# Attention and a quantized network on one core: the scores run one unit further ahead, six product pairs of the network's first group move between attention's last products, and the start and the end are joined differently

## The chip, the core and the metric

The kernel runs on one core of a Trainium2 chip. The core has four engines that compute, each with its own queue of instructions: TensorE (PE; "PEld" is its loading of the stationary operand), VectorE (DVE), ScalarE (ACT) and GpSimd (POOL). SyncE (SP) issues all DMA transfers of this kernel, in one queue. The metric is the time of one execution on the device in microseconds (us); lower is better.

## The reference

Sixteen sequences of 256 tokens with 256 values each go through one attention layer and one network layer, both with the norm before and after and with the input added:

```python
x = x + layernorm(attn(layernorm(x), W_Q, W_K, W_V, W_O, b_Q, b_K, b_V, b_O))
x = x + layernorm(ffn(layernorm(x), gate, up, down))
```

`attn` has 16 heads of 128, a causal mask and a softmax. `ffn` unpacks 4-bit codes with one scale for 32 values into the weights of gate, up (2048 x 256) and down (256 x 2048), and computes `(gelu(x @ gate.T) * (x @ up.T)) @ down.T`. Everything is float32.

## The kernel before

**Precision.** TensorE takes most operands as pairs: a high part (fp32r) and the low rest. A product of two such pairs is three matmuls (high x high, high x low, low x high), which `mm3` (line 353) issues. Six matmuls of 512 columns are the common piece of work ("a product" below).

**Order.** `run` (line 95) issues every instruction behind all issued before it, so each engine's queue has the order of the program, and all instructions have line 99 in the profile; they are told apart by their tiles. `dma` (line 86) does the same for SP, with line 91. Small jobs (norms, unpacking of weights) are generators in lanes; at places called `slot` (line 133) one step of the first lane whose step is for the wanted engine is put into the program. `finish`, `await_` and the loops in `product` (line 762) and `f_get` (line 666) force steps when the data is needed.

**Attention.** Tokens are handled in 8 blocks of 512 (two sequences). For each block, its 16 heads are 16 units: 128 units in all, two to a pair. The main loop (line 952) runs `i` from -4. In iteration i it issues, in this order: scores of unit i+3 (`st_s`, tiles sc, pr), queries and keys of unit i+4 (`st_qk`, two products, tiles pk, pq), the 32x32 turn of the probabilities of i+3 (`st_t`, tr), half of the output product of the pair before (`st_o`, po, tile wo), the weighted values of unit i (`st_z`, pz, zh, zl), the split of the probabilities of i+1 (`st_p`, ph, pl), values (`st_v`, pv), and on SP the load of the turned probabilities of i+2 (`st_b`, hop to pt) and the four stores of those of i+3 (`st_w`, tr to hop). Then come weights: in odd iterations wk and wq of pair p+4, in even ones wo of pair p and half of wv of p+4 (line 990). Blocks after the first take their weights, already split, from a copy in HBM that `w_keep` wrote. A block's normed, turned and split tokens are the tile xT (`ln1`, line 231; `first_tokens`, line 245, for the first block).

**Weights of the network.** From pair 7 of the first block on, `f_make` (line 598) unpacks one of 24 pieces at a time in the lane `idle`, on VectorE (codes, sg, t, v), and `f_scale` scales and splits it on GpSimd and ScalarE. `f_load` (line 590) loads the packed codes (tile ld).

**Network.** Blocks are taken two at a time and the products of gate and up are done by a scheme with seven products in place of eight. `x_ops` (line 684) makes seven combinations of the tokens; class `Two` (line 754) has the seven products m1 to m7, each for gate ("g") and up ("u") with three matmuls (tiles pa, pd, pf, pe). Products of one name are a "pair" below. Their sums, GELU and splits wait in the list `pending` and are issued one or two at a time by `part` (line 830); `quarter` (line 841) issues those that a down product needs. There are 32 groups (4 pairs of blocks, 8 groups of 256 hidden values each). The loop at line 1008 issues the products of group k and between them the four down products (`st_d`, line 850) of group k-1, which add up in four banks of PSUM. In attention's last three iterations m1, m2 and m6 of group 0 are issued after the iteration's other work (line 997).

**End.** After the last group each of the last two blocks is copied from PSUM whole, turned on TensorE, normed, added to the input and stored (`end_now`, line 897).

## Time and profile before

| what | value |
| --- | --- |
| time, median of 3 runs | 1543.86 us (1541.33 to 1545.67) |
| profiled execution, its own time | 1548.52 us |
| its span, first to last instruction | 1546.7 us |
| instructions | 25648 |
| busy: PE / PEld / DVE / ACT / POOL | 1510.8 / 1281.4 / 1178.4 / 1033.0 / 810.1 us |
| mean granted TensorE clock | 0.991 |
| moved by DMA | 407.55 MB, mean 263 GB/s |
| first product of attention (pk) | 10.87 us |
| attention's last output product | ends near 1045 us |
| last apply of the norm on DVE | 1541.67 us |

The page of the profile gives the busy time of each engine and, in 40 slices, its share. The view of waits names for each engine and tile what ended its idle time. The timeline lists instructions with start, duration, engine, line, operation, tiles (written <- read) and, in brackets, idle time of the engine before it and what ended it. The table of stretches gives for a stretch of time the busy time of each engine with its count of instructions, then the granted clock of TensorE (1.00 is full speed), the share of time in which the 16 DMA engines moved data, and GB/s.

### The profile page before, as it was taken

The numbers are of one execution on the slowest core, as the hardware profiler recorded it, in microseconds if no ns is written. First come the engines' busy times: TensorE is split into PE (matmuls) and PEld (weight loads), VectorE is DVE, ScalarE is ACT, GpSimd is POOL, SyncE is SP. The second block draws the span as 40 slices with busy tenths as digits, with TensorE's granted clock in tenths as the row PEclk, the third lists the DMA queues.
The fourth block names the chain that finished last, engine by engine and source line by source line (L and its number), as shares of the span: only waits on it lengthen the run. The fifth ranks groups of instructions, "written<-read, shape, count | busy, mean of one in ns | idle before, by whom it ended". The sixth has DMA issues, their size and how long they took to land.

```text
span 1546.7 us, 25648 instructions
## 1 busy us (share of the span) xinstructions
PE 1510.8 (98%) x7792; PEld 1281.4 (83%) x7792; DVE 1178.4 (76%) x2944; ACT 1033.0 (67%) x2600; POOL 810.1 (52%) x1017
## 2 busy tenths in 40 slices
PE   8999999999999999999999999989999999999996
PEld 7888888888888888888888888877788878878884
DVE  6875878788788788878777777847777777787765
ACT  6876667767767676676675777656666665665663
POOL 3754669568667767766866866861420330240100
PEclk9999999999999999999999999989999999999999
DMA  8998899989899999899899889975547456655551
GB/s 276 335 310 257 249 303 302 313 293 300 280 293 317 291 310 296 267 326 309 266 315 294 287 281 322 324 238 204 216 179 275 185 220 212 236 192 214 218 195 42
DMA packets 200411, 407.55 MB, mean 263 GB/s; under 512 B 21457, under 2 KB 128465, under 8 KB 189521
## 3 DMA queue, kind: packets, MB, share of 16 engines
q1 hardware_dynamic: 200272, 405.91, 78.6%
q8 instruction: 62, 1.02, 0.3%
q14 instruction: 77, 0.62, 0.1%
HBM read 294.15 MB, written 111.67 MB: 262 GB/s over the span
## 4 chain that ended last, share of the span: by engine, by line
PE 80%; DMA 6%; DVE 5%; ACT 4%; SPq 2%; issue 1%; POOL 0%; DVEq 0%; POOLq 0%; ACTq 0%
PE pd L99 11%; PE po L99 10%; PE pk L99 10%; PE pv L99 10%; PE pq L99 9%; PE pz L99 9%; PE sc L99 8%; PE pa L99 7%; PE pf L99 5%; DVE sum L99 3%; DMA wo<-wo 2%; PE pe L99 2%; SPq L91 2%; ACT inter L99 1%; DMA hop<-tr 1%
## 5 line engine op out<-in xcount | busy, mean ns | idle before, releaser
L99 POOL TENSOR_SCALAR pr<-pr,rc 128x128 f32<-128x128 f32 (+1 forms) x512 | 251.7, 508 | 80.8 <-DVE rc L99 80.8
L99 POOL TENSOR_TENSOR pl<-pt,ph 128x512 fp32r<-128x512 f32 x128 | 165.3, 1291 | 218.3 <-ACT ph L99 211.8
L99 ACT ACTIVATE pr<-sc,mn 128x128 f32<-128x128 f32 (+1 forms) x512 | 208.9, 421 | 83.1 <-DVE mn L99 81.7
L99 DVE CUSTOM_DVE_ANT_0 sc<-sc,mask 128x128 f32<-128x128 f32 (+1 forms) x512 | 180.7, 373 | 63.5 <-PE sc L99 54.7
L99 PE MATMUL pv<-wv,xT 128*128 128x512 f32 x768 | 208.9, 407 | 0.0
L99 PE MATMUL pd<-inter,wd 128*128 128x512 f32 x768 | 199.5, 393 | 5.2 <-ACT inter L99 4.0
L99 PE MATMUL pk<-xT,wk 128*128 128x512 f32 x768 | 201.5, 398 | 1.6 <-ACT wv L99 1.4
L99 PE MATMUL pq<-xT,wq 128*128 128x512 f32 x768 | 196.4, 391 | 0.0
L99 ACT ACTIVATE zh<-pz,bqk 128x512 fp32r<-128x512 f32 x128 | 88.5, 692 | 160.6 <-PE pz L99 160.6
L99 POOL TENSOR_TENSOR rs<-rs,mhalf 128x4 f32<-128x4 f32 (+1 forms) x33 | 35.1, 1065 | 288.5 <-DVE rs L99 287.2
L99 PEld LDWEIGHTS pd<-inter,wd 128*128 128x128 f32 x768 | 142.3, 188 | 42.5 <-DVE inter L99 7.0
L99 PEld LDWEIGHTS pq<-xT,wq 128*128 128x128 f32 x768 | 144.5, 188 | 32.9
L99 PE MATMUL po<-zh,wo 128*128 128x512 f32 x512 | 160.3, 394 | 8.4 <-DMA wo<-wo 8.4
L99 PEld LDWEIGHTS pk<-xT,wk 128*128 128x128 f32 x768 | 136.5, 190 | 25.5 <-ACT xT L99 1.6
L99 PEld LDWEIGHTS pv<-wv,xT 128*128 128x128 f32 x768 | 135.0, 189 | 23.6
L99 DVE SCALAR_TENSOR_TENSOR zl<-pz,bqk,zh 128x512 fp32r<-128x512 f32 x128 | 95.2, 744 | 76.9 <-ACT zh L99 76.7
L99 ACT COPY part<-pa 128x512 f32<-128x512 f32 x192 | 111.9, 586 | 62.4 <-PE pa L99 59.8
L99 ACT CAST inter<-sum 128x512 fp32r<-128x512 f32 x128 | 80.1, 626 | 101.1 <-DVE sum L99 100.9
L99 DVE TENSOR_TENSOR inter<-sum,inter 128x512 fp32r<-128x512 f32 x128 | 92.1, 720 | 58.9 <-ACT inter L99 56.0
L99 DVE STREAM_TRANSPOSE tr<-pr 128x768 f32<-128x768 f32 x128 | 123.3, 963 | 1.1
L99 PEld LDWEIGHTS po<-zh,wo 128*128 128x128 f32 x512 | 96.1, 189 | 31.1 <-DMA wo<-wo 11.5
L99 DVE SCALAR_TENSOR_TENSOR kl<-pk,bqk,kh 128x512 fp32r<-128x512 f32 x128 | 96.0, 750 | 30.3 <-ACT kr L99 27.1
(139 smaller groups left out, 3792.6 us busy)
## 6 DMA issues: line engine op xcount, KB each, us to landing
hop<-tr SPq DMA_DIRECT2D x512, 96.0 KB
pt<-hop SPq DMA_DIRECT2D x128, 384.0 KB
wk<-wk SPq DMA_DIRECT2D x64, 512.0 KB
wq<-wq SPq DMA_DIRECT2D x64, 512.0 KB
wo<-wo SPq DMA_DIRECT2D x64, 512.0 KB
wu<-fu SPq DMA_DIRECT2D x32, 1024.0 KB
wg<-fg SPq DMA_DIRECT2D x32, 1024.0 KB
wv<-wv SPq DMA_DIRECT2D x56, 512.0 KB
```

The lines of the kernel that those rows point to most:

```text
L91: queue[0] = nc.sync.dma_start(dst, src).ins
L99: ins = op(dst, *args, **kw)
```

## The change

1. *Start.* `first_tokens`: all four norms on VectorE, ahead of the split of wk; the split of wq after the turned tokens. 30 warming transposes in place of 24, and 3 and 6 more behind the turns. The low part of the first wv is made on VectorE. In pk and pq the two matmuls with low tokens come last.
2. *Lead.* The loop starts at i = -5; scores, turn and stores are of unit i+4, queries and keys of i+5, the load of the probabilities of i+3, into three buffers of pt instead of two. wk and wq are loaded in even iterations (the same lead over their use), wo of pair p+1 and wv of p+5 in odd ones.
3. *Unpacking.* The first packed codes are loaded one pair (two iterations) earlier. `code` has three buffers instead of four, and v is not begun before the piece before it has been scaled.
4. *Hand-over.* In attention's last six iterations m1, m2, m6, m5, m7, m3 of group 0 stand in front of the output products and the weighted values; group 0 puts some of its intermediate copies into the buffers of pr and tr.
5. *End.* m4 of the last group goes ahead of two down products of the group before. The last group's four down products go by half blocks of 256 tokens (`st_last`), each copied, turned, normed, added and stored while the next is multiplied; all pending operations are issued first. The last half block is stored in two parts.

The core of the diff:

```diff
 # first_tokens
-        w_split(0, "k")
         xn = wide("xn")
-        nb = ln_shift(*stats[1], 2)
-        for t in range(2):
-            mv, rs = stats[0]
+        for t in range(4):
+            mv, rs = stats[t // 2]
             run(nc.vector.tensor_scalar, ...)
-        for t in range(2):
-            ln_apply_act(xn[:, 2 + t, :], xs[1][:, t, :], nb, stats[1][1], t)
-        w_split(0, "q")
+        w_split(0, "k")
...
+            keep_warm(3 + 3 * hf)
             run(nc.scalar.copy, hi, tp)
             run(nc.vector.tensor_tensor, lo, tp, f(hi), ALU.subtract)
+        w_split(0, "q")
 # mm3, with lows_last=True in st_qk
+        if lows_last:
+            todo = [todo[m] for m in (0, 1, 3, 4, 2, 5)]
 # st_b
-        pt = work.tile([P, 4, 6, 32], F32, tag="pt", name="pt")
+        pt = work.tile([P, 4, 6, 32], F32, tag="pt", name="pt", bufs=3)
 # f_make, f_scale
+        while unscaled:
+            step(made)
+        v = small_tile(BF16, "v")
...
+        unscaled.append((g, n))
...
             run(nc.gpsimd.tensor_tensor, full, v, scb, ALU.mult)
+            unscaled.remove((g, n))
 # the main loop
-    for i in range(-4, N + 2):
+    for i in range(-5, N + 2):
...
-            if b == 0 and g == 7:
+            if b == 0 and g == 6:
                 pieces = [(fg, n) for fg in range(NG) for n in "gud"]
                 f_load(*pieces[0])
+            if b == 0 and g == 7:
                 for m, piece in enumerate(pieces):
...
-            st_s(i + 3)
+            st_s(i + 4)
-            st_qk(i + 4)
+            st_qk(i + 5)
-            st_t(i + 3)
+            st_t(i + 4)
+        if i == N:
+            X[0].pop("last")()
+        if i >= N - 4:
+            part(0, ("m1", "m2", "m6", "m5", "m7", "m3")[i - (N - 4)])
...
-            st_b(i + 2)
+            st_b(i + 3)
-            st_w(i + 3)
+            st_w(i + 4)
         if odd:
+            weights((p + 1, "o"), (p + 5, "v"))
+        else:
             weights((p + 4, "k"), (p + 4, "q"))
-        else:
-            weights((p, "o"), (p + 4, "v"))
...
-        if i >= N - 3:
-            for name in (("m1",), ("m2",), ("m6",), (), ())[i - (N - 3)]:
-                part(0, name)
 # the loop over groups (m5, m7, m3 of group 0 left out here too)
+        if k == NGRP - 1:
+            parts(k, "m4")
         st_d(k - 1, 0, 0)
...
-        parts(k, "m4")
+        if k < NGRP - 1:
+            parts(k, "m4")
         st_d(k - 1, 0, 1)
...
     finish(urgent)
+    finish(behind)
+    st_last()
```

The new end, in its own words: `st_last` issues what is pending, then for n = 0 to 5

```python
            if n < count:
                multiply(n, 0)
            if 0 <= n - 1 < count:
                turn_and_measure(n - 1)
            if n < count:
                multiply(n, 1)
            if n >= 2:
                apply(n - 2)
```

with n counting the half blocks (1,0), (1,1), (0,0), (0,1). `multiply` adds six matmuls of 256 columns to the bank and copies the half to SBUF on ScalarE; `turn_and_measure` does four transposes and the statistics; `apply` is one operation on VectorE and one on ScalarE for each 128 tokens, and the store.

More of the change, by code (lines that the diff above doesn't have):

```diff
@@ L251, in first_tokens @@
             stats.append((yield from ln_stats([xs[hf][:, t, :] for t in range(2)])))
-        w_split(0, "k")
         xn = wide("xn")
-        nb = ln_shift(*stats[1], 2)
-        for t in range(2):
-            mv, rs = stats[0]
+        for t in range(4):
+            mv, rs = stats[t // 2]
             run(
                 nc.vector.tensor_scalar,
-                xn[:, t, :], xs[0][:, t, :], mv[:, t, 0:1], rs[:, t : t + 1], ALU.subtract, ALU.mult,
-            )
-        for t in range(2):
-            ln_apply_act(xn[:, 2 + t, :], xs[1][:, t, :], nb, stats[1][1], t)
-        w_split(0, "q")
+                xn[:, t, :], xs[t // 2][:, t % 2, :], mv[:, t % 2, 0:1], rs[:, t % 2 : t % 2 + 1],
+                ALU.subtract, ALU.mult,
+            )
+        w_split(0, "k")
         xt = XT[1, 0] = work.tile([P, 2, 2, TB], F32R, tag="xT", name="xT", bufs=4)
@@ L312, in w_split @@
         run(nc.scalar.activation, wv_[:, 0], raw, AF.Copy, scale=c)
-        if n in "vo":
+        if n in "vo" and (p, n) != (0, "v"):
             run(nc.gpsimd.tensor_tensor, wv_[:, 1], raw, f(wv_[:, 0]), ALU.subtract)
@@ L351, with mm3 @@
     STATIONARY_LAST = ((0, 0), (0, 1), (1, 0))
-    def mm3(o, terms, passes=STATIONARY_LAST, start=True, stop=True, shared=False):
+    def mm3(o, terms, passes=STATIONARY_LAST, start=True, stop=True, shared=False, lows_last=False):
         todo = [(lhs(a), rhs(c)) for lhs, rhs in terms for a, c in passes]
+        if lows_last:
+            todo = [todo[m] for m in (0, 1, 3, 4, 2, 5)]
         for i, (lhs, rhs) in enumerate(todo):
@@ L378, in st_qk @@
         pk = ps.tile([P, TB], F32, tag="pk", name="pk")
-        mm3(pk, [(lambda a, kt=kt: wk_[:, a, kt, cols], lambda c, kt=kt: xt[:, c, kt, :]) for kt in range(2)], MOVING_LAST)
+        mm3(pk, [(lambda a, kt=kt: wk_[:, a, kt, cols], lambda c, kt=kt: xt[:, c, kt, :]) for kt in range(2)], MOVING_LAST, lows_last=True)
         kh = work.tile([P, TB], F32R, tag="kh", name="kh")
@@ L389, in st_qk @@
         pq = ps.tile([P, TB], F32, tag="pq", name="pq")
-        mm3(pq, [(lambda a, kt=kt: wq_[:, a, kt, cols], lambda c, kt=kt: xt[:, c, kt, :]) for kt in range(2)], MOVING_LAST)
+        mm3(pq, [(lambda a, kt=kt: wq_[:, a, kt, cols], lambda c, kt=kt: xt[:, c, kt, :]) for kt in range(2)], MOVING_LAST, lows_last=True)
         qh = work.tile([P, 2, P], F32R, tag="qh", name="qh")
@@ L588 @@
     LD = {}
+    unscaled = []
     def f_load(g, n):
@@ L603, in small_tile @@
         def small_tile(dtype, name):
-            return work.tile([P, 2, 256], dtype, tag="code", name=name, bufs=4)
+            return work.tile([P, 2, 256], dtype, tag="code", name=name, bufs=3)
         c = work.tile([P, 2, 256], I32, tag="raw", name="codes", bufs=6)
-        sg, t, v = small_tile(BF16, "sg"), small_tile(BF16, "t"), small_tile(BF16, "v")
+        sg, t = small_tile(BF16, "sg"), small_tile(BF16, "t")
         run(nc.vector.tensor_scalar, c[:, 0, :], pk, 15, None, ALU.bitwise_and)
@@ L638, in f_scale @@
             run(nc.gpsimd.tensor_tensor, full[:, 0:4].rearrange("p (k c) n -> p k (c n)", k=2), v, scb, ALU.mult)
+            unscaled.remove((g, n))
             w = f_tile("u")
@@ L770, in copy @@
         def copy(self, bank, tag, bufs=2):
-            t = sb_tile(tag, "part", bufs)
+            if self.k == 0 and tag in ("zh", "zl"):
+                t = work.tile([P, 3, D], F32, tag="pr" if tag == "zh" else "tr", name="part").rearrange("p a b -> p (a b)")
+                t = t[:, 0:TB]
+            else:
+                t = sb_tile(tag, "part", bufs)
             run(nc.scalar.copy, t, bank)
@@ L868, in st_d @@
         if g == NG - 1:
-            if sb < NSB - 1:
-                if dh == 0:
-                    ACC[b] = back_tile()
-                back(ACC[b], dh, po)
-                if dh == 1:
-                    add((urgent, behind)[bb], end(b, ACC.pop(b)), N_)
-            else:
-                if dh == 0:
-                    ACC[b] = wide("oT").rearrange("p a b -> p (a b)").rearrange("p (h n) -> p h n", h=2)
-                run(nc.scalar.copy, ACC[b][:, dh], po)
-                if dh == 1:
-                    add(urgent, end_now(b, ACC.pop(b), tags), V_)
+            if dh == 0:
+                ACC[b] = back_tile()
+            back(ACC[b], dh, po)
+            if dh == 1:
+                add((urgent, behind)[bb], end(b, ACC.pop(b)), N_)
     def end(b, tr):
@@ L895, in end, with st_last, multiply, turn_and_measure @@
             dma(half(out, b, hf), X1[b][hf])
-    def end_now(b, oT, tags):
-        yield V_
-        tp = []
-        for hf in range(2):
-            tp.append(ps.tile([P, 2, D], F32, tag=tags[hf], name="tpo"))
+    def st_last():
+        k = NGRP - 1
+        while pending:
+            run(*pending.popleft())
+        w = FW[k, "d"]
+        halves = [(bb, hf) for bb in (1, 0) for hf in range(2)]
+        oTs, os, stats = {}, {}, {}
+        def multiply(n, dh):
+            bb, hf = halves[n]
+            tok = slice(hf * S, (hf + 1) * S)
+            cols = slice(dh * P, (dh + 1) * P)
+            i = [quarter(k, c, bb) for c in range(2)]
+            po = ACC[2 * NSB - 2 + bb, dh][:, tok]
+            mm3(
+                po, [(lambda a, c=c: w[:, a, c, cols], lambda s, c=c: i[c][:, s, tok]) for c in range(2)], MOVING_LAST,
+                start=False, shared=True,
+            )
+            if dh == 0:
+                oTs[n] = wide("oT").rearrange("p a b -> p (a b)")[:, 0 : 2 * S].rearrange("p (h n) -> p h n", h=2)
+            run(nc.scalar.copy, oTs[n][:, dh], po)
+        def turn_and_measure(n):
+            tp = ps.tile([P, 2, D], F32, tag=("pk", "pq", "sc", "sc")[n], name="tpo", bufs=2 if n > 1 else 1)
+            oT = oTs.pop(n)
             for t in range(2):
@@ L906, in end_now, with measure, apply @@
                         nc.tensor.transpose,
-                        tp[hf][:, t, dh * P : (dh + 1) * P], oT[:, dh, (2 * hf + t) * P : (2 * hf + t + 1) * P], ident,
+                        tp[:, t, dh * P : (dh + 1) * P], oT[:, dh, t * P : (t + 1) * P], ident,
                     )
-        o = [tp[t // 2][:, t % 2, :] for t in range(4)]
-        mv, rs = yield from ln_stats(o)
-        nb = ln_shift(mv, rs, 4)
-        fa = wide("fa")
-        for t in range(2):
-            ln_apply_act(fa[:, t, :], o[t], nb, rs, t)
-        for t in range(2, 4):
-            run(
-                nc.vector.tensor_scalar,
-                fa[:, t, :], o[t], mv[:, t, 0:1], rs[:, t : t + 1], ALU.subtract, ALU.mult,
-            )
-        for hf in (1, 0):
-            run(nc.vector.tensor_tensor, X1[b][hf], X1[b][hf], fa[:, 2 * hf : 2 * hf + 2, :], ALU.add)
-            dma(half(out, b, hf), X1[b][hf])
+            os[n] = [tp[:, t, :] for t in range(2)]
+            jobs = deque()
+            stats[n] = None
+            def measure():
+                stats[n] = yield from ln_stats(os[n])
+            add(jobs, measure(), V_)
+            finish(jobs)
+        def apply(n):
+            bb, hf = halves[n]
+            b = 2 * NSB - 2 + bb
+            mv, rs = stats.pop(n)
+            nb = ln_shift(mv, rs, 2)
+            x1 = X1[b][hf]
+            for t in range(2):
+                run(
+                    nc.vector.scalar_tensor_tensor,
+                    x1[:, t, :], os[n][t], rs[:, t : t + 1], x1[:, t, :], ALU.mult, ALU.add,
+                )
+                run(nc.scalar.activation, x1[:, t, :], x1[:, t, :], AF.Identity, bias=nb[:, t : t + 1])
+                if n == len(halves) - 1:
+                    dma(half(out, b, hf)[:, t, :], x1[:, t, :])
+            if n < len(halves) - 1:
+                dma(half(out, b, hf), x1)
+        count = len(halves)
+        for n in range(count + 2):
+            if n < count:
[6 more added lines that the diff above has]
+                apply(n - 2)
     first = first_tokens()
@@ L936, with keep_warm @@
     warm = ps.tile([P, 4, P], F32, tag="pz", name="warm")
-    for n in range(24):
-        run(nc.tensor.transpose, warm[:, n % 4, :], ident, ident)
+    def keep_warm(count):
+        for n in range(count):
+            run(nc.tensor.transpose, warm[:, n % 4, :], ident, ident)
+    keep_warm(30)
     add(urgent, first, V_)
@@ L965 @@
                 add(spare, x_ops(0), N_)
-        if 0 <= i + 3 < N:
-            st_s(i + 3)
+        if 0 <= i + 4 < N:
+            st_s(i + 4)
         slot(V_)
-        if i + 4 < N:
-            st_qk(i + 4)
+        if i + 5 < N:
+            st_qk(i + 5)
         slot(V_, urgent, behind)
@@ L973 @@
         slot(G_)
-        if 0 <= i + 3 < N:
-            st_t(i + 3)
+        if 0 <= i + 4 < N:
+            st_t(i + 4)
[3 more added lines that the diff above has]
+            part(0, ("m1", "m2", "m6", "m5", "m7", "m3")[i - (N - 4)])
         if 0 <= p - 1 < len(pairs):
@@ L981 @@
             st_p(i + 1)
-        if i + 4 < N:
+        if 0 <= i + 4 < N:
             st_v(i + 4)
@@ L985 @@
             run(*after.popleft())
-        if 0 <= i + 2 < N:
-            st_b(i + 2)
         if 0 <= i + 3 < N:
-            st_w(i + 3)
+            st_b(i + 3)
+        if 0 <= i + 4 < N:
+            st_w(i + 4)
         if odd:
+            weights((p + 1, "o"), (p + 5, "v"))
+        else:
             weights((p + 4, "k"), (p + 4, "q"))
-        else:
-            weights((p, "o"), (p + 4, "v"))
         slot(A_ + G_)
@@ L1005, in parts @@
             part(k, name)
-    X[0].pop("last")()
-    for k in range(NGRP + 1):
+    for k in range(NGRP):
         sb, g = divmod(k, NG)
-        if k < NGRP:
-            if g == 2 and sb + 1 < NSB:
-                while not {(0, 2 * sb + 2), (0, 2 * sb + 3)} <= ready:
-                    step(behind)
-                add(spare, x_ops(sb + 1), N_)
-            if g == NG - 1:
-                for b in (2 * sb, 2 * sb + 1):
-                    X1[b] = [x_load(x1d, b, hf, ("pr", "tr")[b % 2]) for hf in range(2)]
+        if g == 2 and sb + 1 < NSB:
+            while not {(0, 2 * sb + 2), (0, 2 * sb + 3)} <= ready:
+                step(behind)
+            add(spare, x_ops(sb + 1), N_)
+        if g == NG - 1:
+            for b in (2 * sb, 2 * sb + 1):
+                X1[b] = [x_load(x1d, b, hf, ("pr", "tr")[b % 2]) for hf in range(2)]
         if k > 0:
@@ L1026 @@
             parts(k, "m6")
-        parts(k, "m5")
+            parts(k, "m5")
         slot(V_)
@@ L1032 @@
         slot(A_ + G_)
-        parts(k, "m7", "m3")
+        if k > 0:
+            parts(k, "m7", "m3")
+        if k == NGRP - 1:
+            parts(k, "m4")
         st_d(k - 1, 0, 0)
```

## The prediction

> **What bounds the kernel now.** The page first: TensorE (PE) is busy for 98% of the span and makes 80% of the chain that ended last. So work on other engines is worth nothing unless PE waits for it, and the change removes no product. What can be won is PE's idle time, 1546.7 - 1510.8 = 35.9 us, and the time in which PE has half its clock.

> ```profile
> span 1546.7 us, 25648 instructions
> ...
> PE 1510.8 (98%) x7792; PEld 1281.4 (83%) x7792; DVE 1178.4 (76%) x2944; ACT 1033.0 (67%) x2600; POOL 810.1 (52%) x1017
> ...
> PEclk9999999999999999999999999989999999999999
> ```

> Next the waits of PE: who was waited for, total us, times, longest.

> ```profile
> PE po L99 <- DMA wo<-wo: 8.4, 6, 4.1
> PE pd L99 <- ACT inter L99: 4.0, 4, 1.9
> PE sc L99 <- DVE kl L99: 2.3, 1, 2.3
> PE sc L99 <- ACT qr L99: 1.8, 2, 1.1
> ```

> Four places show: the load of wo, the end (inter), one stop at kl, the start (qr); the longest wo wait is in the hand-over to the network. Then a table of stretches cut at the clock's steps (busy us of PE, PEld, DVE, ACT, POOL; granted clock; DMA share; GB/s):

> ```profile
> 10.38:13.80 3.42, 2.93 (x7) 2.38 (x8) 0.94 (x2) 1.02 (x2) 2.51 (x2) 0.50 0.98 373
> 150.33:153.74 3.41, 1.12 (x6) 0.69 (x5) 2.01 (x7) 1.40 (x3) 1.35 (x3) 1.00 0.53 162
> 153.74:157.15 3.41, 3.40 (x12) 2.98 (x12) 3.07 (x11) 1.02 (x5) 2.11 (x2) 0.50 0.46 99
> ...
> 1024.14:1027.56 3.42, 3.42 (x13) 3.03 (x14) 0.75 (x1) 0.69 (x1) 1.00 (x1) 0.50 0.76 203
> ...
> 1030.97:1037.80 6.83, 5.61 (x18) 4.93 (x19) 0.00 (x0) 0.61 (x2) 1.17 (x1) 0.50 1.03 418
> ```

> A stretch in which PE stood (1.12 us busy of 3.41) is followed by one at clock 0.50, and half of what PE does there is lost: 1.5 at the start, 1.7 after 153.74, 1.7 after 846.65 (same answer), 1.7 + 2.8 in the hand-over; 9.4 us in all. A stop of 2.3 us thus costs 4.

> [...] Here gaps of 2.29 and 2.21 us already halve the next stretch. [...]

> **The change, part by part.** In the steady part a unit of attention takes 7.83 us (pk starts at 243.68 and 251.51), all of it PE. That stays: the same products, the same engine orders but for the shift. Using the low tokens last in pk and pq is free there.

> *wo is loaded a step earlier.* Before, it is issued at the end of an even iteration and used two iterations on; now at the end of the odd one before: 7.83 us more. On SP it stands behind the same hop writes, and its tile was last read by that iteration's output products, so nothing new holds it. The waits outside the hand-over are 0.74 at 214, 0.28 at 356, 0.78 at 592, 0.27 at 608 and 2.21 at 846: 4.3, plus 1.7 of clock: 6.0. All are shorter than 7.83 and go. The load of the probabilities moves alike (three buffers of pt); ScalarE waits 37.0 us in all for it, but in the steady part PE never does: nothing.

> *Packed codes are loaded two iterations earlier.*

> ```profile
> 151.73 0.49 DVE L99 TENSOR_SCALAR codes<-ld 128x256 int32<-128x256 int32 x2 [5.90 <-DMA ld<-in_gp]
> ...
> 153.40 0.38 PE L99 MATMUL sc<-kl,qh 128*128 128x256 f32 x1 [2.29 <-DVE kl L99]
> ```

> VectorE stood 5.90 us for a load issued in the same iteration, kl was queued behind, and PE stood for kl. Two iterations are 15.7 us, so this goes: 2.3 + 1.7 = 4.0. Three code buffers instead of four let the next piece's v wait for GpSimd's scaling; in the built order that scaling mostly stands a unit or more ahead, so nothing, at worst one more such stop (4.0). Steady part together: -10.0, from -6.0 to -10.3 (the last 0.24, xT of block 1 at 129, should stay).

> *Start.* VectorE does all four norms (0.37 each, 0.73 for two); its rs at 6.04 and 7.02 give xn at 7.1 and 7.9, and wk's low part at 8.6. Thirty warming transposes from 1.56, 0.224 each (5.38 for 24) and faster after the clock's step at 6.97, end near 7.6; transposes, three warming, transposes, six warming end near 9.5, as do xT's high halves (0.52 each). So pk starts at 9.5 instead of 10.87: 1.4. With PE full up to 10.38 the half clock goes: 1.5. Against it, qk runs five units ahead: the first scores come straight after the first qk and wait for kh, kr, qh, qr (0.69 + 3 x 0.47) behind wv's halves (1.16): ready at 13.4, pq done at 12.3, idle 1.1. And there is a fourth round of scores, qk, pv (5.3 us of PE, in rounds that took 6.2 and 6.6) before the first z: 0.8. Net -1.0, from +1.0 (the 1.1 us halve the clock, one full round is lost) to -2.5.

> *Hand-over.* From 1008 to 1056:

> ```profile
> 1008.00:1056.00 48.00, 41.82 (x193) 33.87 (x192) 24.91 (x52) 27.42 (x58) 22.06 (x23) 0.89 0.66 208
> ```

> PE is busy 41.8 of 48: 6.2 idle, with 4.5 of clock 10.7. Now each of the last six iterations has a pair of products (1.36) before its output products (1.36) and z (1.17), 3.9 us. From the start of the last scores, the last z comes 5.1 (rest of that iteration) + 3 x 3.9 + 2.7 = 19.5 us later. Its chain: scores to scaled probabilities 5.0 (1016.60 to 1021.55), transpose 1.0, hop writes 1.9 to 3.8 to issue and about 4 to land, load about 5.4, ph 0.6, pl 1.3: 19.2 to 21.1. And from z over zh (0.69), ph (0.61) and pl (1.29), 2.6 must fit in 2.7. Just: I leave 1.5 us idle (0.5 to 6.0, the upper end today's) and no clock step: -9.2, from -4.7 to -10.2. The load queued behind the stores of turned tokens (1.8 on SP) is inside these ends. ScalarE has some 17 us of work in 25.

> *End.* After the group before the last (1523.2) 23.5 us follow:

> ```profile
> 1524.52 3.97 PE L99 MATMUL pd<-inter,wd 128*128 128x512 f32 x15 [1.19 <-ACT inter L99]
> ...
> 1530.39 1.23 PE L99 MATMUL pd<-inter,wd 128*128 128x512 f32 x3 [1.90 <-ACT inter L99]
> ```

> The last GELU was queued on ScalarE behind two copies of pd, and the norm of a block began when all of it was there. Now m4 goes in front of two d products; but its two banks are free only when VectorE has read pf (1519.3, 1520.5), 1.0 of new waiting, and VectorE's row of sums is then as long as before: inter is ready near 1524.4, no sooner. What goes is the stop at 1530.39. By half blocks (0.7 each product, copies 0.45, four transposes 0.45, statistics and aggregates 1.1, POOL 0.72, two applies 1.0 each on VectorE and ScalarE) the last copies end near 1533.9, the last statistics near 1535.7, the last apply near 1538.8, against 1542.96 (1541.67 + 1.29) now. The writes then take 3.7 as now (to 1546.7): -4.2, from -2.0 to -5.5.

> **Sum.** -10.0 - 1.0 - 9.2 - 4.2 = -24.4; the ends add up to -11.7 and -28.5. The profiled execution took 1548.5 (span 1546.7): 1524.1. It is 4.7 slower than the median, 1543.86; the runs spread over 4.3, and what stalls most is what this change removes, so I cannot subtract all of the 24.4 from the median (1519.5) nor keep all of the 4.7 (1524.1): **1522.0**, between the two.

> **Rivals.** *The hand-over stays tight.* The last load comes late behind the token stores, PE stands, and the clock halves: hand-over -4.7, start +1.0, so 6.5 less gained: 1528.5. For it: 19.5 against up to 21.1, and 2.6 against 2.7; against it: DMA is only 0.66 busy there. *The steady stalls are the profiled run's.* If the measured runs have only half of the 10.0, or half comes back behind VectorE: 1527. Against it: five waits in one run, and a load issued in the iteration that uses it. *The edit of wo does nothing,* since SP stands on another wait ahead of it: 6.0 less, 1528; but the steady iterations show SP reaching that load each time. *Slower.* qk of a new block runs one iteration sooner and finds xT missing at seven block boundaries. In the built order block 1's second half still stands right before that qk, as it did with a wait of 0.24; the other blocks' stand three units ahead. Half an iteration each (3.9), and 1.7 of clock, would cost 7 x 5.6 = 39: 1561. It decides from 24.4/7 = 3.5 us a boundary on.

> **Chances.** Forecast 0.73 (own range 1515 to 1527); tight hand-over 0.11, half the steady stalls 0.07, wo without effect 0.04: all faster, 0.95. Slower 0.03. The remaining 0.02 is no change, 0.3% being about what a measurement of this kernel can tell from none. The range reaches from 1514.5, a little beyond 1543.9 - 28.5 = 1515.4, to 1530.5, a little above the first rival; 1543.9 - 11.7 = 1532.2, all bounds bad at once, is left out.

> **What will show it.** In the changed profile: no wait of po for wo and none of codes for ld; clock 0.50 in no stretch after the start; pk from about 9.5 and first scores near 13.4; idle of PE under 2 us in the last six iterations; no stop of inter between the last d products, and last applies about 4 us sooner after the last full group. Wrong would be: pz waiting for pl or ph in the last iterations, a half clock after the first scores, pk waiting for xT at block boundaries, or VectorE standing at v for GpSimd.

## The result, and the profile after

The changed kernel takes 1521.91 us (median of 4 runs, 1520.87 to 1523.28). The kernel before took 1543.46 in the same comparison (4 runs, 1541.33 to 1545.67). The ratio is 0.9861, 95% interval 0.9844 to 0.9878. The forecast was 1522.0.

The profiled execution took 1522.04 us, its span is 1520.3. The page, in the places shown of before:

```profile
span 1520.3 us, 25782 instructions
...
PE 1501.7 (99%) x7831; PEld 1278.5 (84%) x7831; DVE 1175.9 (77%) x2950; ACT 1033.9 (68%) x2606; POOL 810.3 (53%) x1018
...
PEclk9999999999999999999999999999999999999999
```

PE is still the bound. Its idle time fell from 35.9 to 18.6 us (1520.3 - 1501.7), and the dent in the row of the clock is gone. PE's busy time fell by 9.1 us although it has 39 instructions more: matmuls at half the clock count as busy for nearly twice as long (the six of the first product 2.90 us in experiment 8, 1.63 here). The waits of PE after (who was waited for: total us, times, longest):

```profile
PE sc L99 <- ACT qr L99: 5.4, 4, 2.2
PE warm L99 <- POOL ident masks.py:199: 1.6, 1, 1.6
PE pd L99 <- DVE inter L99: 1.4, 5, 0.3
PE pd L99 <- ACT inter L99: 1.2, 3, 0.4
PE pz L99 <- POOL pl L99: 0.9, 1, 0.9
```

The waits of po for wo (8.4) and of sc for kl (2.3) are gone, the long one for inter too. One row grew: sc waits for qr 5.4 us in place of 1.8; all of that is in the start. Three stretches after (busy us of PE, PEld, DVE, ACT, POOL; clock; DMA share; GB/s):

```profile
142.00:158.00 16.00, 16.00 (x91) 13.93 (x90) 11.50 (x37) 10.91 (x32) 7.50 (x11) 1.00 0.84 262
832.00:850.00 18.00, 18.00 (x100) 15.56 (x99) 14.93 (x49) 13.77 (x42) 13.77 (x21) 1.00 0.89 305
1000.00:1034.00 34.00, 32.98 (x176) 27.84 (x175) 24.15 (x38) 22.05 (x43) 22.75 (x20) 1.00 0.72 243
```

The first two hold the places where before stood for codes and for wo: PE has no gap now. The third is the hand-over: 1.0 us idle of 34 at full clock, where before had 6.2 of 48 and a clock of 0.89. No wait of VectorE at v for GpSimd is in the trace, which the forecast had named as a sign of being wrong.

**By stages.** I cut each trace at four marks: the first scores of unit 8, of unit 127, the first product of group 1, the end. The second column of before is a second profiled execution of it (first experiment). In the changed kernel the scores of a unit come one iteration sooner in the order, so 3.93 us of PE's work that before had done by the scores of unit 8 (half an output product, one pz, one pv) comes behind those of unit 127; the table counts it back into the start.

| stage, us | before | before, second | after | forecast of the change |
| --- | --- | --- | --- | --- |
| start, to scores of unit 8 | 71.76 | 72.31 | 73.45 (69.52 + 3.93) | -1.0 |
| steady, to scores of unit 127 | 944.84 | 938.98 | 932.69 | -10.0 |
| hand-over, to m1 of group 1 | 35.21 | 34.92 | 25.06 (28.99 - 3.93) | -9.2 |
| rest of the network and end | 494.89 | 494.89 | 489.10 | -4.2 |
| span | 1546.7 | 1541.1 | 1520.3 | -24.4 |

### The profile page after: what moved, and what is told of

Read it like the earlier page. It is cut to its first block, busy times and chain, and to the rows that moved or that the text cites. A ratio compares the mean times of both kernels' runs of the same rounds, so it can differ in the third digit from the quotient of the medians.

```text
span 1520.3 us, 25782 instructions
## 1 busy us (share of the span) xinstructions
PE 1501.7 (99%) x7831; PEld 1278.5 (84%) x7831; DVE 1175.9 (77%) x2950; ACT 1033.9 (68%) x2606; POOL 810.3 (53%) x1018
## 3 DMA queue, kind: packets, MB, share of 16 engines
q8 instruction: 62, 1.02, 0.3%
## 4 chain that ended last, share of the span: by engine, by line
PE 89%; DVE 5%; ACT 4%; DMA 1%; issue 1%; POOL 1%; POOLq 0%; ACTq 0%; SPq 0%; DVEq 0%
PE pd L99 11%; PE pk L99 11%; PE po L99 11%; PE pv L99 11%; PE pq L99 11%; PE pz L99 10%; PE sc L99 9%; PE pa L99 7%; PE pf L99 5%; DVE sum L99 3%; PE pe L99 2%; DVE inter L99 1%; ACT inter L99 1%; ACT part L99 1%; ACT o L99 1%
## 5 line engine op out<-in xcount | busy, mean ns | idle before, releaser
L99 POOL TENSOR_SCALAR pr<-pr,rc 128x128 f32<-128x128 f32 (+1 forms) x512 | 250.2, 504 | 89.9 <-DVE rc L99 89.9
L99 ACT ACTIVATE pr<-sc,mn 128x128 f32<-128x128 f32 (+1 forms) x512 | 208.2, 419 | 87.2 <-DVE mn L99 87.0
L99 POOL TENSOR_TENSOR pl<-pt,ph 128x512 fp32r<-128x512 f32 x128 | 165.0, 1289 | 190.1 <-ACT ph L99 181.8
L99 DVE CUSTOM_DVE_ANT_0 sc<-sc,mask 128x128 f32<-128x128 f32 (+1 forms) x512 | 180.6, 373 | 67.8 <-PE sc L99 59.1
L99 PE MATMUL pv<-wv,xT 128*128 128x512 f32 x768 | 208.9, 407 | 0.0
L99 PE MATMUL pd<-inter,wd 128*128 128x512 f32 (+1 forms) x792 | 199.7, 386 | 2.7 <-DVE inter L99 1.4
L99 ACT ACTIVATE zh<-pz,bqk 128x512 fp32r<-128x512 f32 x128 | 88.3, 690 | 167.3 <-PE pz L99 167.2
L99 PE MATMUL pk<-xT,wk 128*128 128x512 f32 x768 | 199.4, 395 | 0.3 <-POOL xT L99 0.2
L99 PE MATMUL pq<-xT,wq 128*128 128x512 f32 x768 | 196.3, 391 | 0.0
L99 POOL TENSOR_TENSOR rs<-rs,mhalf 128x4 f32<-128x4 f32 (+1 forms) x35 | 35.9, 1026 | 283.9 <-DVE rs L99 277.5
L99 PEld LDWEIGHTS pd<-inter,wd 128*128 128x128 f32 x792 | 144.2, 188 | 38.6 <-DVE inter L99 6.5
L99 PEld LDWEIGHTS pq<-xT,wq 128*128 128x128 f32 x768 | 144.2, 188 | 32.8
L99 PE MATMUL po<-zh,wo 128*128 128x512 f32 x512 | 157.7, 389 | 0.0
L99 PEld LDWEIGHTS pk<-xT,wk 128*128 128x128 f32 x768 | 134.9, 188 | 23.8 <-POOL xT L99 0.7
L99 PEld LDWEIGHTS pv<-wv,xT 128*128 128x128 f32 x768 | 135.0, 189 | 23.6
L99 ACT COPY part<-pa 128x512 f32<-128x512 f32 x192 | 111.5, 584 | 62.7 <-PE pa L99 60.3
L99 DVE SCALAR_TENSOR_TENSOR zl<-pz,bqk,zh 128x512 fp32r<-128x512 f32 x128 | 95.8, 749 | 73.7 <-ACT zh L99 73.6
L99 ACT CAST inter<-sum 128x512 fp32r<-128x512 f32 x128 | 80.1, 626 | 100.0 <-DVE sum L99 99.9
L99 DVE TENSOR_TENSOR inter<-sum,inter 128x512 fp32r<-128x512 f32 x128 | 93.2, 728 | 58.9 <-ACT inter L99 56.0
L99 DVE STREAM_TRANSPOSE tr<-pr 128x768 f32<-128x768 f32 x128 | 123.3, 963 | 1.7 <-POOL pr L99 1.2
L99 DVE SCALAR_TENSOR_TENSOR kl<-pk,bqk,kh 128x512 fp32r<-128x512 f32 x128 | 96.1, 751 | 30.7 <-ACT kr L99 26.7
L99 PEld LDWEIGHTS po<-zh,wo 128*128 128x128 f32 x512 | 96.0, 188 | 19.9
```

The source lines that it names most:

```text
L99: ins = op(dst, *args, **kw)
```

## The experiments

All kernels are the changed one with the edit shown, but for the first. Times are medians with the range of the runs; to compare: changed 1521.9, before 1542.3 to 1544.2 in the three groups of runs. The time of the changed kernel is that of the result above, from a group of its own with before. As ratios to before, numbers 4, 5, 8, 11 and 12 overlap with its interval, so these differences of 0.4 to 2.8 us rest on the stages of the traces. An iteration is named by the unit whose queries and keys it makes.

**1. The kernel before, profiled again.** No edit.

> The kernel before once more, for a second profile. Theory A (the stops for wo and ld are the program's own): the same sums in the same places, 12.3 us of iterations beyond 7.83 between the scores of unit 8 and of unit 127 within 1.5 us, however long this execution takes. Theory B (part of them belonged to the one profiled execution, which was 4.7 us above the median): in an execution near 1543.5 us the steady part shows about 5 us less, that is about 7.5.

It took 1542.92 us. PE's waits in this second profile of before:

```profile
PE po L99 <- DMA wo<-wo: 6.6, 3, 5.7
PE pd L99 <- ACT inter L99: 3.9, 4, 1.9
...
PE sc L99 <- DVE kl L99: 2.3, 1, 2.3
```

Theory B. The stop at kl is the same (iteration of unit 19: 12.28 us, 4.45 over 7.83; in the first profile 4.38). Of wo, 5.7 is the one stop in the hand-over, and what is left in the steady part cost 1.8 us (938.98 - 4.45, less the 932.69 that the changed kernel takes without either stop) instead of 7.8 (944.84 - 4.38 - 932.69). That difference of 6 us is what set the first profiled execution 5.6 us apart from this one. So the waits for wo vary from execution to execution. In 37 runs of the kernel before, beside the experiments, the time lay between 1539.1 and 1551.5.

**2. wo late, behind wk and wq.**

```diff
         if odd:
-            weights((p + 1, "o"), (p + 5, "v"))
+            weights((p + 5, "v"))
         else:
-            weights((p + 4, "k"), (p + 4, "q"))
+            weights((p + 4, "k"), (p + 4, "q"), (p, "o"))
```

> The changed kernel with wo of pair p loaded in the even iteration of pair p again, behind wk and wq; all else as changed. Theory A (each wait for wo costs what the traces show, 7.9 us in the steady part): about 1529.8 us, waits of po for wo of 5 to 9 us back in the trace. Theory B (half of the cost belonged to the one profiled execution): about 1526. Rival (with the longer lead nothing waits for wo any more, the gain came from elsewhere): 1522, no wait for wo over 0.3 us.

1552.07 us (1548.34 to 1556.59; the profiled execution was the fastest), 30 more than changed and slower than before (1.0051, 1.0034 to 1.0068). None of the theories had this. PE stands 12.7 us at wo in 9 stops. One of them, first on SP's queue (the issue of each load), then on PE:

```profile
335.20 1.75 SPq L91 DMA_DIRECT2D xhop<-xtr  x4
337.62 0.34 SPq L91 DMA_DIRECT2D o<-ohop  x1
338.00 0.96 SPq L91 DMA_DIRECT2D xs<-in_x  x2
339.06 0.41 SPq L91 DMA_DIRECT2D pt<-hop  x1
339.57 1.82 SPq L91 DMA_DIRECT2D hop<-tr  x4
341.74 0.34 SPq L91 DMA_DIRECT2D wk<-wk  x1
342.42 0.34 SPq L91 DMA_DIRECT2D wq<-wq  x1
343.28 0.32 SPq L91 DMA_DIRECT2D wo<-wo  x1
```

```profile
350.98 0.73 PE L99 MATMUL po<-zh,wo 128*128 128x512 f32 x2 [2.34 <-DMA wo<-wo]
```

wo is issued at 343.28 and PE goes on at 350.98: 7.7 us for 512 KB; in this iteration, once a block, the tokens of other blocks, the probabilities, wk and wq were issued just ahead of it. The DMA share was 1.05 in these 7.7 us, 0.84 in the 8.3 us before; whether the order in the queue or the shared engines made wo late is not separated. Such iterations (units 27, 43, 75, 91) took 11.9 to 12.5 us instead of 7.83, the stop and a stretch at half clock (behind the stop shown, three matmuls of pz took 0.42 us each, in the changed kernel 0.28); in units 59, 107 and 123 they took 8.3 to 8.8. Unit 16 lost 4.8 more to a stop for xT, as in number 3. So the load of wo has little margin in an even iteration, where before had it too.

**3. wo late, ahead of wk and wq** (its iteration as before).

```diff
         if odd:
-            weights((p + 1, "o"), (p + 5, "v"))
+            weights((p + 5, "v"))
         else:
-            weights((p + 4, "k"), (p + 4, "q"))
+            weights((p, "o"), (p + 4, "k"), (p + 4, "q"))
```

> The changed kernel with wo of pair p loaded in the even iteration of pair p, as before, but ahead of wk and wq (the run with wo behind them took 1552). Theory A (the load has to go through in one and a half iterations and mostly does; the second profile of the kernel before lost 1.8 us at wo in the steady part, the first 7.9, and both lost 6.0 in the hand-over): 1527 to 1536 us, spread of 3 us or more between executions, and waits of po for wo in the steady part and in the hand-over. Rival (with its longer lead the changed kernel has no such stops, and only the place behind two large loads made them): 1522 to 1524.

1528.69 us (1528.01 to 1531.83): 6.8 more, as Theory A had it, but not for its reason. The trace has wo waits of 1.4 us in all. Most is at unit 16 (12.94 us):

```profile
124.06 0.63 ACT L99 ACTIVATE wo<-rawo 128x512 fp32r<-128x512 f32 x1
...
126.73 0.62 ACT L99 CAST xT<-xr 128x512 fp32r<-128x512 f32 x1
```

```profile
127.41 0.96 PE L99 MATMUL pk<-xT,wk 128*128 128x512 f32 x3 [2.25 <-ACT xT L99]
129.25 0.79 PE L99 MATMUL pk<-xT,wk 128*128 128x512 f32 x1 [0.88 <-POOL xT L99]
```

In the first block wo is split on chip, and that job stands ahead of the split of block 1's xT in the slots. Three weights in one iteration pushed xT back, 4.6 us. The loads themselves cost 1.0 (unit 29) and 0.9 in the hand-over. This is the forecast's slower rival, xT missing at a block boundary, at one boundary, made by another edit.

**4. Codes late.**

```diff
-            if b == 0 and g == 6:
+            if b == 0 and g == 7:
                 pieces = [(fg, n) for fg in range(NG) for n in "gud"]
                 f_load(*pieces[0])
```

> The changed kernel with the first packed codes loaded in the iteration that uses them, as before. Theory A (one stop of VectorE, 4.4 us of PE's time with the half clock behind it): about 1526.3 us, codes waits for ld by 5 to 6 us. Rival (scores are now a unit further ahead, so the stop of VectorE is absorbed before PE needs kl): 1522 to 1523, with the wait of codes in the trace but no stop of PE.

1524.23 us (1521.95 to 1525.37): 2.3 more. VectorE, then PE, at the place:

```profile
155.35 0.50 DVE L99 TENSOR_SCALAR codes<-ld 128x256 int32<-128x256 int32 x2 [4.75 <-DMA ld<-in_gp]
...
157.03 0.38 PE L99 MATMUL sc<-kl,qh 128*128 128x256 f32 x1 [1.14 <-DVE kl L99]
```

Between the theories: VectorE stands nearly as long as before (5.90 there), PE half as long (2.29), and the clock stays at 1.00; the iteration is 1.7 us longer instead of 4.4. The rest of the 2.3 is not this stop: in the profiled execution PE also stood 1.53 us for wu in the network (see number 9).

**5. Old hand-over.**

```diff
-        if i == N:
-            X[0].pop("last")()
-        if i >= N - 4:
-            part(0, ("m1", "m2", "m6", "m5", "m7", "m3")[i - (N - 4)])
...
+        if i >= N - 3:
+            for name in (("m1",), ("m2",), ("m6",), (), ())[i - (N - 3)]:
+                part(0, name)
```

(m5, m7, m3 of group 0 and the tiles of its copies are also as before.)

> The changed kernel with the products of group 0 where they were before (m1, m2, m6 behind the last three iterations, the rest after attention); scores still a unit further ahead. Theory A (the hand-over's 10.2 us come from the six product pairs that give PE work between the last weighted values): 1528 to 1532 us, PE idle 4 us or more between 1000 and 1036 and a clock of 0.50 there. Rival (they come from the longer lead, the probabilities being ready earlier): 1522 to 1525, PE idle under 2 us there.

1524.75 us (1524.50 to 1525.09), 2.8 more. The time is the rival's; PE's idle, 3.1 us from 1000 to 1036 at full clock, lies between the two. That the lead is the reason, as the rival had it, does not hold (table under number 7). The stage takes 32.39 us against 28.99. The stops on PE are those that the forecast's chain named, pl and zl, and they are short:

```profile
1008.57 0.50 PE L99 MATMUL po<-zl,wo 128*128 128x512 f32 x1 [0.67 <-DVE zl L99]
...
1010.59 0.38 PE L99 MATMUL pz<-pl,vh 128*128 128x256 f32 x1 [1.29 <-POOL pl L99]
```

**6. Old lead, and 7. old lead with old hand-over.** Number 7 is number 6 with the edit of number 5.

```diff
-    for i in range(-5, N + 2):
+    for i in range(-4, N + 2):
...
-            st_s(i + 4)
+            st_s(i + 3)
...
-            st_qk(i + 5)
+            st_qk(i + 4)
...
-            st_t(i + 4)
+            st_t(i + 3)
...
-            st_b(i + 3)
+            st_b(i + 2)
...
-            st_w(i + 4)
+            st_w(i + 3)
         if odd:
-            weights((p + 1, "o"), (p + 5, "v"))
+            weights((p + 1, "o"), (p + 4, "k"), (p + 4, "q"))
         else:
-            weights((p + 4, "k"), (p + 4, "q"))
+            weights((p + 4, "v"))
```

> The changed kernel with the old lead (scores of unit i+3, queries and keys of i+4, probabilities loaded for i+2; wk and wq loaded in odd iterations, half of wv in even ones, wo a step earlier as changed). The product pairs still move. Theory A (the lead is what the hand-over needs: with the pairs undone but the lead kept only 3.4 of its 10.2 us came back): the other 4 to 7 us come back, less 1.7 for the shorter start: 1524 to 1527 us. Rival (the earlier load of wo, not the lead, took the long stop of the hand-over away): the hand-over loses under 1.5 us, the start gains 1.7: 1520 to 1521.7.

> The run before this one with the product pairs of group 0 at their old place as well: old lead, old hand-over, the rest (loads of wo and codes, start, end) changed. If lead and moved pairs add up: 2.8 us above the run with the old lead alone. If one stands in for the other: 5 us or more above it, 1527 to 1530, near all of the hand-over's 10.2 us but for the 4 to 6 of wo. If wo's load was all: within 2.8 us of 1521.9.

1532.51 us (1530.04 to 1536.31) and 1534.50 (1530.93 to 1537.30), both outside what was expected. The totals say little of the lead, for my order of loads, three in one iteration, cost 7.0 and 10.6 us in the steady part, where pk again stood 2.2 us for xT at unit 16. The hand-over can be read by itself (us from the scores of unit 127 to m1 of group 1, with 3.93 added for the old lead):

| lead | products of group 0 | wo | stage |
| --- | --- | --- | --- |
| 4 | old | late (before, two profiles) | 39.1, 38.9 |
| 4 | old | early (number 7) | 33.1 |
| 4 | moved | early (number 6) | 30.0 |
| 5 | old | early (number 5) | 32.4 |
| 5 | moved | early (changed) | 29.0 |
| 5 | moved | late, first (number 3) | 29.9 |

Read from before to number 7, 6 and the changed kernel, loading wo earlier brings 6.0 of the 10 us (number 7 has no stop at wo there; before had one of 4.1 and of 5.7), moving the products 3.1 more, the lead 1.0 more. Read by way of number 3, products and lead bring 9.2 or 9.0 with wo still late, and the early load then 0.9, for the products run while wo lands. So the effects are not sums: each of the two removes most of the stop alone.

The lead hardly pays by itself in these two stages. It brings 0.7 (number 5 against 7) or 1.0 in the hand-over. In the start, numbers 6 and 7 reach the scores of unit 8 at 72.1 and 71.5, the kernels with the longer lead at 72.7 in the mean (68.7 + 3.93), though 6 and 7 stand 1.4 and 1.1 us there for qr. In the steady part late codes cost 1.7 us with it (number 4) and 4.4 in before.

**8. Old start.**

```diff
-            keep_warm(3 + 3 * hf)
...
-    keep_warm(30)
+    keep_warm(24)
```

(and two norms on ScalarE behind the split of wk, wq's split ahead of the turns, the low part of the first wv on GpSimd, as before.)

> The changed kernel with the start as before: two norms on ScalarE behind the split of wk, 24 warming transposes, none between the turns. Theory A (first product 0.9 us later and one stretch of 3.41 us at half the clock): 1523.5 to 1524.5 us, first product at 10.9. Rival (the first scores wait for ScalarE and for loads anyway, which hide a later first product): 1522 to 1522.7.

1524.06 us (1523.27 to 1524.82), 2.2 more: the time is Theory A's. On PE:

```profile
8.48 1.35 PE L99 MATMUL tpx<-ident,xn 128*128 128x128 f32 x8 [1.53 <-DVE xn L99]
11.22 2.90 PE L99 MATMUL pk<-xT,wk 128*128 128x512 f32 x6 [1.39 <-ACT wv L99]
```

The first product of the changed kernel:

```profile
9.94 1.63 PE L99 MATMUL pk<-xT,wk 128*128 128x512 f32 x6
```

Two gaps, and the first product takes 2.90 us at half clock, against 1.63 in the changed kernel; in before it took the same 2.90, at a granted clock of 0.50. But the rival is in part right: from the first product to the scores of unit 8 it takes 59.6 us here and 59.1 to 59.6 in the six traces with the new start (the changed kernel and numbers 2 to 5 and 9). The second scores wait 0.76 us for qr instead of 1.60 to 2.18, which hides most of the half clock. What shows at unit 8, 2.1 us (70.81 against 68.7 in the mean), is mostly the later first product: 11.22 against 8.88 to 9.94.

**9. Old end.**

```diff
-        if k == NGRP - 1:
-            parts(k, "m4")
         st_d(k - 1, 0, 0)
...
-    finish(behind)
-    st_last()
```

(`end_now` for whole blocks again.)

> The changed kernel with the end as before: m4 of the last group in its old place, the last two blocks copied, turned and normed whole. Theory A (the traces put 6.2 us on the end): 1528.1 us, within 0.7. Rival (some of the 6.2 came from earlier, pending operations issued at once or less work left over): 1526 or less.

1529.29 us (1528.67 to 1532.16), 7.4 more: Theory A, a little above it. From m7 of group 31 to the end it takes 30.7 us (before 30.3, changed 24.2; so 6.5 of the 7.4), with the old stops:

```profile
1507.64 3.94 PE L99 MATMUL pd<-inter,wd 128*128 128x512 f32 x15 [1.19 <-ACT inter L99]
1513.48 1.52 PE L99 MATMUL pd<-inter,wd 128*128 128x512 f32 x3 [1.90 <-ACT inter L99]
1519.21 0.98 PE L99 MATMUL tpo<-ident,oT 128*128 128x128 f32 x7 [0.57 <-ACT oT L99]
```

The profiled execution was the slowest of the four (1532.16), and this has to do with another place:

```profile
1049.65 1.38 PE L99 MATMUL pa<-xT,wu 128*128 128x512 f32 x3 [1.56 <-DMA wu<-fu]
```

With 1.13 us for wg just before, PE stood 2.7 us for weights of the network behind the hand-over, and the three matmuls shown took 1.38 us, where such three take 0.84 in the changed kernel at full clock. Five of the ten traces with the products of group 0 moved have such a stop near 1050 (numbers 3, 4, 6, 9, 12: 0.3 to 2.7 us), the changed kernel's has none, and none of the four with the old order has one (both of before, numbers 5 and 7). So the moved products seem to have left these loads little margin, which no experiment tested.

**10. Splits later in the start.** In the changed kernel ScalarE, then PE, in the second round:

```profile
16.75 0.63 ACT L99 ACTIVATE wv<-rawv 128x512 fp32r<-128x512 f32 x1 [2.88 <-DMA rawv<-in_wv]
...
21.75 0.49 PE L99 MATMUL sc<-kr,qr 128*128 128x128 f32 x2 [2.18 <-ACT qr L99]
```

VectorE had the last minimum of unit 0 at 16.6 and the first near 15.3, but the exponentials stood behind the split of a wv that is needed four rounds later.

```diff
-    for p, n in (2, "v"), (1, "k"), (1, "q"):
-        w_get(p, n)
...
+        if i == -4:
+            w_get(1, "k")
+            w_get(1, "q")
...
+        if i == -3:
+            w_get(2, "v")
```

> The changed kernel with the splits of the second pair's wk and wq issued after the first scores and that of the third wv two iterations later, so that the exponentials of unit 0 are not queued on ScalarE behind a load that lands at 16.7 us. Theory A (the 2.88 us that ScalarE stood for that load are what made PE stand 2.2 us for qr): 1519.5 to 1520.5 us, the second scores at about 19.7 instead of 21.75. Rival (ScalarE's own work in a round, exponentials, splits and copies, is as long as the wait): 1521.5 or more, PE still waiting 1.5 us or more for qr there.

1520.61 us (1519.79 to 1521.52), 0.1 above Theory A's range. The second scores:

```profile
19.11 0.49 PE L99 MATMUL sc<-kr,qr 128*128 128x128 f32 x2 [0.76 <-ACT qr L99]
```

The scores of unit 8 come at 66.92 (changed 69.52, and 67.94 to 68.88 in numbers 2 to 5 and 9, which start alike). The ratio to before, 0.9845 (0.9814 to 0.9875), overlaps that of the changed kernel, so its 1.3 us in the median are shown by the trace's start, not by the times alone. There, 58.2 us lie between the first product and the scores of unit 8, in the six others 59.1 to 59.6: 0.9 to 1.4 us are the edit's, the rest an earlier first product (8.74).

**11. Values a round sooner,** on top of number 10.

```diff
-        if 0 <= i + 4 < N:
+        if 0 <= i + 5 < 4:
+            st_v(i + 5)
+        elif 4 <= i + 4 < N:
             st_v(i + 4)
```

> The run before this one, with the values of block 0's first four parts each one round sooner, so that a product stands between the first queries and the first scores. Theory A (PE's wait of 1 us before the first scores is filled, the total work is the same): 0.5 to 1.0 us below the run before this one. Rival (the wait only moves: the copies of pv come ahead of the exponentials on ScalarE, or the round without values is then short of work): same as the run before this one within 0.4 us, or above it.

1522.28 us (1520.31 to 1523.19): nothing won, the rival. The wait before the first scores is filled, but its time comes back: the scores of unit 4, in the round that has lost its values, now wait 2.44 us for qr. The scores of unit 8 come at 67.61, 0.7 later than in number 10, and so does the first product (9.38 against 8.74); between the two lie 58.2 us in both.

**12. Splits of wk and wq ahead of the exponentials,** on top of number 10.

```diff
+        if i < 0:
+            while splits and splits[0][2] == V_:
+                step(splits)
         if 0 <= i + 4 < N:
             st_s(i + 4)
+        while lows:
+            run(*lows.popleft())
```

(`lows` holds the low parts of pairs 1 and 2.)

> The run with the later splits (1520.6) with one more edit: the high parts of wk and wq of pairs 1 and 2 are made on ScalarE ahead of the exponentials of units 0 and 1, where ScalarE stood 2.0 and 1.7 us for VectorE's minima, and the low parts on VectorE behind those minima. Theory A (a start round is bound by the chain scores, minima, exponentials, splits, keys and queries; 1.2 us of it go in two rounds): 1518.8 to 1519.8 us, no wait of PE over 0.3 at the second and third scores. Rival (the packed weights' raw loads land later than the minima are ready, or the gain stays inside what other waits in the start take back): 1520.3 or more.

1523.34 us (1522.28 to 1524.77): worse than number 10. The second and third scores came at 18.69 and 25.30, but my loop also pulled the splits of pair 3 ahead of the scores of unit 3, with their low parts on VectorE in front of that unit's minima; PE then stood:

```profile
39.20 0.49 PE L99 MATMUL sc<-kr,qr 128*128 128x128 f32 x2 [2.36 <-ACT qr L99]
```

From 40.28 to 43.69 the granted clock was 0.50. What was won in two rounds was lost in those after: from the first product to the scores of unit 8 it takes 60.3 us, 2.1 more than in number 10.

## Why the forecast held, step by step

- *Steady part, -10.0.* Against the first profile -12.15 came out, beyond the term's bounds of -6.0 to -10.3, against the second -6.3. Codes were sized right: 4.0 forecast, 4.4 measured in both. wo was forecast at 6.0; it cost 7.8 in the first profile (PE's idle was counted, not what an iteration lost beyond it: the one with the stop of 0.74 at 214 was 1.03 longer) and 1.8 in the second. The forecast knew this case: its second rival, stalls that are the profiled run's, is what happened. Its price of 1527 did not follow, for other terms were larger.
- *Hand-over, -9.2.* -10.15 and -9.9: right in size, half right in its cause. The forecast put all of it on the pairs of products and the longer lead, and these do bring 9.0 to 9.2 without the early wo (number 3). But it priced wo only outside the hand-over, and there the early load alone brings 6.0 (number 7): one stop, removed twice. The stop that it expected, pz for pl in the last iterations, is there with 0.88 us.
- *Start, -1.0.* +1.7 in the profiled pair, outside the forecast's bounds; with the six traces that start alike (scores of unit 8 at 68.7 in the mean, against 72.0 in the mean of the two profiles of before) +0.6. Two steps failed, as number 8 tells, which has the old start with the new lead. First, the gain: first product and half clock bring 2.1 (70.81 to 68.7) where 1.4 + 1.5 was forecast, for most of the half clock's price was hidden by waits for qr. Second, the price of the lead, "idle 1.1" and 0.8 for the fourth round: with all else that differs up to unit 8 it is 2.7 (70.81 + 3.93 against 72.0). PE waited 0.99, 2.18, 1.06 and 1.12 us in four rounds. Working from PE's rounds, it left out ScalarE's queue: exponentials, splits and the copies of keys and queries are one chain with the scores, and a late load stood in front of them (number 10).
- *End, -4.2.* -6.2 in the trace from m7 of the last group on (the 31 groups before it took 0.4 more, hence -5.8 in the table), 7.4 in the times of number 9. All three lie beyond the term's bounds of -2.0 to -5.5. The order was as forecast, the times shorter: m4 waited 0.24 us at 1500.33 and 0.1 before it, where 1.0 was forecast, and pd waited 0.23 for inter. Put beside before by m7 of the last group (20.23 us earlier), PE's last turn began at 1532.9, where the copies were forecast to end at 1533.9; the last applies ended at 1537.5 instead of 1538.8, and the writes then took 3.1 instead of 3.7.

The end in the changed kernel, with PE's last turn and the last applies:

```profile
1504.88 2.50 PE L99 MATMUL pd<-inter,wd 128*128 128x256 f32 x16 [0.23 <-DVE inter L99]
...
1512.66 0.82 PE L99 MATMUL tpo<-ident,oT 128*128 128x128 f32 x4 [0.40 <-ACT oT L99]
...
1515.31 1.92 ACT L99 ACTIVATE xs<-xs,nb 128x256 f32<-128x256 f32 x4 [1.03 <-DVE xs L99]
1515.80 0.88 DVE L99 SCALAR_TENSOR_TENSOR xs<-tpo,rs,xs 128x256 f32<-128x256 f32 x2
```

- *The sum.* The choice between 1519.5 and 1524.1 was the right kind of doubt: the profiled execution of before was 5 us above its median, and nearly all of it was waiting for wo. Against the second profile the stages give +1.1 - 6.3 - 9.9 - 5.8 = -20.8 (rounded), which is the difference of the spans. Between the medians of the result lie 21.6 us of the 24.4 summed. That 1522.0 agrees to 0.1 us is partly luck: start 1.6 to 2.7 us too good, end 2 too poor, wo between its two sizes.

What stays open: why the same start takes 67.9 us to the scores of unit 8 in one execution and 69.5 in another (1.06 of the 1.6 us lie ahead of the first product, at 8.88 and at 9.94); what a lead of 4 would give with its loads spread well; what the three code buffers and the order of the low tokens do by themselves; and how often wg and wu come late. No run separates these.

## What to carry to other kernels

A wait that an engine shows in one profiled run may be a margin and not a cost: profile the kernel twice before pricing it, and ask of each load what else is issued just ahead of it at the fullest moment, since 512 KB landed 7.7 us after its issue there. Undoing parts of a change one at a time shows what each still protects, not what it brought: here moved work and an early load cover the same stop (the load brings 6.0 alone, 0.9 beside the other). Behind work that was moved ahead, look for the next load that it makes late, as wu seems to be here. Where work is shifted further ahead, price the start by the longest chain through all engines' queues, and look there for an operation that waits for data not yet needed.

## What the runs showed of the hardware

In these traces the clock did not go by the length of a gap alone. The changed kernel's gap of 2.18 us (19.57 to 21.75) fell on two stretches of the raster, and the clock stayed at 1.00; PE alone (busy, instructions, clock, DMA share, GB/s):

```profile
17.89:21.30 3.41, 1.67 (x8) 1.00 0.59 175
21.30:24.72 3.42, 2.97 (x18) 1.00 0.84 268
```

In the kernel before, in the hand-over, a stretch with a gap of 1.49 us was followed by half the clock:

```profile
1020.73:1024.15 3.42, 1.79 (x8) 1.00 0.51 122
1024.15:1027.56 3.41, 3.41 (x13) 0.50 0.76 204
```

These are the stretches of the raster in those two traces, from the first step that is recorded (6.97 and 7.65), that have work of PE behind them. In before, five at full clock were followed by a clock of 0.50: with PE busy for 1.35 us (from 6.97), 1.12 (150.33), 1.20 (843.24), 1.79 (1020.73) and 0.55 (1027.56). So was one with 1.08 in number 12 (36.86). The one with 1.67 in the changed kernel was not, nor was any other, all with over 2.2. Why 1.79 was and 1.67 was not, no run shows; the ends of matmuls are modelled in these figures. At a clock of 0.50, one stretch with 2.20 us busy (1030.97 in before) was followed by another such; 2.93 (10.38) and 3.41 (153.74, 846.65, 1024.15, 1034.39) were followed by full clock.
